# Attention with its score and weighing matmuls in blocks of eight, values stored twice, short scalings on ScalarE, memory reordered, and the third item's operands given a home of their own

## The chip, the cores and the metric

The kernel runs on one core of a Trainium2 chip. The metric is the device time of one launch in microseconds. Engines are called as in the profile: PE is TensorE, DVE is VectorE, ACT is ScalarE, POOL is GpSimd, SP is SyncE (here it only issues DMAs).

## The reference, cut to what matters

Four batch items of 512 tokens, 1024 features, all in float32. After a layer norm the result is the sum of three things: x itself, an attention with ALiBi-like bias, and a linear layer with a low-rank part chosen by a router.

```
qkv = xn @ w_qkv                       # 32 query heads, 8 key/value heads of 128
scores = einsum(q, k) * 128 ** -0.5    # 4 query heads share one key/value head
bias = -slope * sqrt(max(i - j, 0)), -inf for j > i
attn = softmax(scores + bias)
out = attn @ v, then @ w_o
ffn = xn @ W.T + b + routed low-rank part
x + out + ffn
```

## The kernel before, in words

The kernel has three stages on one core. Matrix products are done by a two-level Strassen scheme (seven products for eight), so operands are needed as sums and differences of quarters; DVE and POOL make these.

**Projection** (`project`, matmuls on line 569). It makes q, k and v for all heads and stores them in DRAM. Values of two heads are transposed and stored by `put` (lines 597 to 602), four DMAs of 32 partitions. Beside the matmuls, one call of `beside` at a time, `weights_put_by` (from line 784) loads pieces of the weights through ACT's queue, makes sums of them on DVE or POOL (line 827) and stores them through SP's queue (line 836). `pause(n)` in it lets n turns go by. The order of PE, SP, DVE and POOL is that of the program.

**Attention** (`attend`). A unit is one batch item and one key/value head: 32 units, four steps T each, 128 steps (`STEPS`). All engines and SP's queue work in program order, so the loop over T from line 1217 is the schedule. In step T:

- `scores(T)` (line 1047): four score matmuls of 128 query rows (32 positions of four heads) against 32 to 512 keys, lines 1053 on PE. Each has one of four PSUM banks. DVE adds the bias and takes the row's extreme (line 1058, frees the bank), ACT takes the exponential and its sum (line 1061).
- `scaled(T - 1)` (line 1071): the four probability rows are multiplied by the inverse of their sums, on POOL. Of the four, two are long (288 to 512) and two short (32 to 256).
- `turn(T - 2)`: DVE transposes the step's probabilities in blocks of 32 (line 1084).
- `weigh(T - 6)` (line 1113): probabilities times values, 24 rounds' matmuls of 32 rows of the array each, four at a time (line 1100). The results of a unit stand in four PSUM banks.
- every four steps `settle` (line 1120) copies them out on ACT (line 1127).
- `aside(beside, ...)` and `aside(below, ...)` take the next of the operand sums that the last stage needs: `outer_sums` on POOL, `middle_sums` on DVE where `kept` (items 1 and 2) or of `os` (5, 6, 3), on POOL for 7 and 4. They end in DMA stores to `s_d` through SP's queue (lines 1172 to 1186), for the last pair of heads partly through POOL's (line 1168). `below` advances by one or two sums a step in turn.
- `load` brings q and k of the next unit; `values` (line 1030) brings v of this unit, four DMAs of 32 partitions from the same source, since the weighing needs v on each quarter of the partitions.

In step 112 the first operands of the last stage are loaded (`front[0]`), in step 130 the second item's (`second_home`), and `begin` puts the first matmuls of the last stage between the last weighings. After the loop come the sums of the last pair.

**Last stage** (`finish`, matmuls on line 1371). 49 items (7 outer times 7 inner products); an item needs four operand quarters `sa00` to `sa11`, its weights `w` and sums of them (`tokens`, `weights`). Operands of item n + 2 are loaded while item n runs (`beside`, slots 2 to 6). Item 0 is done without the inner scheme; ACT copies its results into the tile `u` (line 1394).

Pools lie in memory as stacks. The pool `b` of the attention and the pool `c2` of the last stage start at the same place, so where a tag stands in the list of line 1215 decides which tile of the attention a tile of the last stage must wait for. Offsets in words of a partition, worked out from the sizes in the code, before: ot1 16128 to 18176, vy to 20224, pty to 24832; in `c2` t4 15872 to 17152, u 17152 to 19200.

Of the kernel before, what the change touches and what calls it, by code (L numbers as in the profile page):

```python
# [66 lines left out]
def kernel(  # L67
# [58 lines left out]
    v_d = {(i, h): scratch(f"v{i}_{h}", [2, 32, P // 32, NT, D]) for i in range(B) for h in range(0, NKV, 2)}  # L126
# [238 lines left out]
    def project(attention):  # L365
# [5 lines left out]
        with pool("a") as sb, tc.tile_pool(name="stats", bufs=2, reuse_waits="tile") as stats:  # L371
# [182 lines left out]
            def item(st, i, acc):  # L554
# [30 lines left out]
                def put(t, row, col):  # L585
                    bi = 2 * p + row
                    if kind == "q":
                        src = t.rearrange("p a b -> p (a b)").rearrange("p (j f) -> p j f", f=2 * C)
                        dst = q_d[bi, h].rearrange("p j g k -> p j (g k)")
                        nc.sync.dma_start(out=dst[:, :, ts(col, 2 * C)], in_=src)  # L590
                    elif col == 0:
                        nc.sync.dma_start(out=k_d[bi, h], in_=t)
                    else:
                        for j in range(2):
                            tr = bank("tr", f"v_{n}_{j}")
                            for c in range(NT):
                                nc.tensor.transpose(tr[:, ts(c, P)], t[:, j, ts(c, P)], ident)
                            nc.scalar.copy(t[:, j], tr)
                        dst = v_d[bi, h].rearrange("j k g c d -> g k j (c d)")
                        in_while(4, lambda: [  # L600
                            nc.sync.dma_start(out=dst[g], in_=t[ts(g, 32)]) for g in range(P // 32)
                        ])
# [181 lines left out]
            def weights_put_by(turn):  # L784
# [31 lines left out]
                for n in range(turn, len(pieces), 3):  # L816
                    key, eng = pieces[n], (GP, V)[n % 2]
                    if len(key) == 2 and key[1] in SUMMED:
                        while not put_by >= {(key[0], e, j) for e in range(2) for j in range(2)}:
                            yield  # L820
                    w = load(key)
                    yield from pause(8)
                    for k, u, v in ((0, 1, 0), (1, 3, 1), (3, 3, 0), (2, 2, 3)):
                        while busy(eng):
                            yield
                        taken[eng] = pace[2]
                        pin(sub(eng, w[:, k], w[:, u], w[:, v]))
# [143 lines left out]
    def attend(front, begin):  # L971
# [3 lines left out]
        with ExitStack() as stack:  # L975
# [177 lines left out]
            def middle_sums(p, h, which, of, t, kept):  # L1153
# [27 lines left out]
                for k in range(g):  # L1181
                    if kept:
                        nc.sync.dma_start(out=d[k][:, 1], in_=s3[:, k])
                    else:
                        queue.dma_start(out=d[k][:, :4], in_=a[:, k].rearrange("p e r k -> p (e r) k"))
                    queue.dma_start(out=d[k][:, 4:], in_=m[:, :3, k])
                yield

            beside, below = deque(), deque()
# [71 lines left out]
            p, h = last  # L1261
            cuts = [(ALL, slice(HS, S)), (ALL, slice(0, HS))]
# [157 lines left out]
    def finish(sb, homes, ops, begun):  # L1420
# [16 lines left out]
        for tags, shape, n in (  # L1437
            ("x", [NP, 2, HS], 4), ("btb", [DOUT], 1), ("um", [NP, S], 1), ("lw", [12, P], 1),
            ("r4", [2, NP, HS], 8), ("t4", [KB, P], 2), ("u", [2, NP, HS], 2),
            ("m1 m5 m6", [HS], 2), ("wz", [2 * KB, HS], 1), ("sa10z sa11z", [KB, HS], 1),  # L1440
            ("s2 s4", [KB, HS], 2), ("t3", [KB, P], 2),
# [203 lines left out]
        def beside(n, slot):  # L1645
# [57 lines left out]
    homes, begun = [], {}  # L1703
    ops = {n: None for n in range(2)}

    def lay(home, k):

        for tag, shape in (
# [3 lines left out]
            home.tile([P, *shape], F32, tag=tag, name=f"lay_{tag}_{k}")  # L1712
# [10 lines left out]
    def second_home(o):  # L1723
# [7 lines left out]
        bring(1, "w", (0, 1))  # L1731

# [59 lines left out]
```

## Time and profile before

| | us |
|---|---|
| median of 3 runs | 2530.95 (2528.68 to 2532.22) |
| the profiled execution | 2529.27 |
| its span | 2527.5 |

| engine | busy us | share of the span |
|---|---|---|
| PE | 2450.1 | 97% |
| weight loads (PEld) | 2082.3 | 82% |
| DVE | 1802.9 | 71% |
| POOL | 1929.3 | 76% |
| ACT | 516.0 | 20% |

DMA moved 681.90 MB, 270 GB/s on average. The projection takes the first 1143 us of the span, the attention lasts to some 1722, the last stage from there.

A busy share is the mean over stages with different limits, so stretches of the span are read one by one. In a line of instructions, the name behind "<-" in brackets is what ended the idle time ahead of the instruction. A matmul in float32 stands as two records (two passes). The DMA share is the mean busy share of 16 DMA engines; it is over 1 where packets overlap. The granted clock is 1.00 at full speed.

### The profile page before, as it was taken

The numbers are of one execution on the slowest core, as the hardware profiler recorded it, in microseconds if no ns is written. First come the engines' busy times: TensorE is split into PE (matmuls) and PEld (weight loads), VectorE is DVE, ScalarE is ACT, GpSimd is POOL, SyncE is SP. The second block draws the span as 40 slices with busy tenths as digits, with TensorE's granted clock in tenths as the row PEclk, the third lists the DMA queues.
The fourth block names the chain that finished last, engine by engine and source line by source line (L and its number), as shares of the span: only waits on it lengthen the run. The fifth ranks groups of instructions, "written<-read, shape, count | busy, mean of one in ns | idle before, by whom it ended". The sixth has DMA issues, their size and how long they took to land.

```text
span 2527.5 us, 44178 instructions
## 1 busy us (share of the span) xinstructions
PE 2450.1 (97%) x16096; PEld 2082.3 (82%) x16096; DVE 1802.9 (71%) x3586; ACT 516.0 (20%) x1558; POOL 1929.3 (76%) x2078
## 2 busy tenths in 40 slices
PE   7999999999999999999999999997999999999999
PEld 6878888888888888887777777775888888888887
DVE  7776677778666676757899998975765666656574
ACT  3111111110000000116666666641000000000000
POOL 4578787887688898875999999975775667747583
PEclk9999999999999999999999999998999999999999
DMA  4389998878977777746899999999887877879884
GB/s 146 109 246 318 281 323 253 271 220 245 323 226 241 217 243 223 247 136 183 248 319 326 319 331 320 321 304 356 317 317 268 327 288 289 307 267 329 312 325 149
DMA packets 513834, 681.90 MB, mean 270 GB/s; under 512 B 155817, under 2 KB 424489, under 8 KB 499410
## 3 DMA queue, kind: packets, MB, share of 16 engines
q1 hardware_dynamic: 441554, 591.64, 71.5%
q10 hardware_dynamic: 70752, 82.85, 9.9%
q0 software_dynamic: 1312, 4.59, 0.5%
q8 instruction: 128, 2.10, 0.3%
q14 instruction: 88, 0.72, 0.1%
HBM read 417.89 MB, written 261.10 MB: 269 GB/s over the span
## 4 chain that ended last, share of the span: by engine, by line
PE 67%; DMA 3%; POOL 2%; DVE 1%; SPq 1%; issue 1%; ACT 0%; ACTq 0%; DVEq 0%; POOLq 0%
PE pc L1371 16%; PE po L1100 11%; PE psc L1053 10%; PE pd L1371 8%; PE pc_q L569 7%; PE pa L1371 4%; PE pd_q L569 3%; PE pc_kv L569 3%; PE pa_q L569 2%; PE pd_kv L569 2%; DMA sa<-s 1%; PE pa_kv L569 1%; POOL t L140 1%; POOL ti_q L140 1%; PE pc L1635 1%
## 5 line engine op out<-in xcount | busy, mean ns | idle before, releaser
L1100 PE MATMUL po<-pt,v 32*128 32x256 f32 (+7 forms) x6144 | 300.1, 334 | 5.1 <-DMA v<-v 4.4
L1061 ACT ACTIVATE p<-p,low 128x512 f32<-128x512 f32 (+15 forms) x512 | 261.4, 517 | 203.7 <-DVE low L1058 195.7
L1100 PEld LDWEIGHTS po<-pt,v 32*128 32x128 f32 x6144 | 266.1, 186 | 36.3 <-issue 23.7
L1073 POOL TENSOR_SCALAR p<-p,tot 128x512 f32<-128x512 f32 (+15 forms) x512 | 264.3, 534 | 41.3 <-DVE tot L1069 40.8
L1053 PE MATMUL psc<-k,q 128*128 128x512 f32 (+15 forms) x1024 | 279.4, 417 | 3.0 <-DVE low L1058 2.5
L140 POOL TENSOR_TENSOR t<-w 128x640 f32<-128x640 f32 x95 | 187.9, 1978 | 120.9 <-DMA w<-m 54.6
L1058 DVE CUSTOM_DVE_ANT_0 p<-psc,bias 128x512 f32<-128x512 f32 (+15 forms) x512 | 205.6, 435 | 69.5 <-PE psc L1053 66.1
L1053 PEld LDWEIGHTS psc<-k,q 128*128 128x128 f32 x1024 | 171.5, 191 | 96.6 <-issue 55.8
L140 POOL TENSOR_TENSOR t<-w,t 128x640 f32<-128x640 f32 x95 | 194.8, 2051 | 33.9 <-PE pc L1371 30.2
L140 POOL TENSOR_TENSOR wr<-wr 128x256 f32<-128x256 f32 x220 | 174.6, 795 | 47.2 <-DMA wr<-in_w_o_dram 21.6
L569 PE MATMUL pc_q<-xi,ti_q 128*128 128x256 f32 x640 | 167.6, 385 | 3.0 <-DVE q L137 2.7
L1084 DVE STREAM_TRANSPOSE pt<-p 128x1088 f32<-128x1088 f32 x128 | 167.0, 1305 | 1.7 <-POOL p L1073 1.7
L140 POOL TENSOR_TENSOR ti_q<-w_q 128x256 f32<-128x256 f32 x128 | 105.3, 822 | 67.7 <-PE pc_q L569 37.4
L140 DVE TENSOR_TENSOR wr<-wr 128x256 f32<-128x256 f32 x220 | 139.5, 634 | 14.0 <-DMA wr<-in_wt_dram 9.1
L569 PEld LDWEIGHTS pc_q<-xi,ti_q 128*128 128x128 f32 x640 | 121.4, 192 | 24.3 <-issue 4.9
L569 PE MATMUL pd_q<-xi,ti_q 128*128 128x256 f32 x448 | 117.6, 386 | 14.6 <-POOL ti_q L140 14.6
L179 ACT COPY m<-pc 128x256 f32<-128x256 f32 x30 | 11.2, 372 | 564.1 <-PE pc L1371 545.1
L1371 PE MATMUL pc<-s,t 128*128 128x256 f32 x480 | 113.3, 384 | 10.5 <-DVE m L137 10.5
L140 POOL TENSOR_TENSOR ti_q<-to_q 128x256 f32<-128x256 f32 x96 | 76.8, 800 | 47.5 <-PE pc_q L569 45.0
L1371 PE MATMUL pc<-sa,w 128*128 128x256 f32 x480 | 112.1, 381 | 0.1
L1371 PEld LDWEIGHTS pc<-s,t 128*128 128x128 f32 x480 | 92.4, 193 | 23.6 <-issue 10.9
L1371 PE MATMUL pd<-s,t 128*128 128x256 f32 x480 | 111.5, 379 | 0.0
(344 smaller groups left out, 5731.1 us busy)
## 6 DMA issues: line engine op xcount, KB each, us to landing
sa<-s SPq DMA_DIRECT2D x98, 640.0 KB, 7.9
s<-ot SPq DMA_DIRECT2D x107, 384.0 KB, 6.1
m<-wr SPq DMA_DIRECT2D x70, 512.0 KB, 4.1
w<-m SPq DMA_DIRECT2D x28, 1280.0 KB, 8.1
w_q<-in_w_qkv_dram SPq DMA_DIRECT2D x16, 2048.0 KB, 11.3
q<-q SPq DMA_DIRECT2D x32, 1024.0 KB, 5.7
v<-v SPq DMA_DIRECT2D x128, 256.0 KB, 5.9
s<-os SPq DMA_DIRECT2D x45, 512.0 KB, 6.1
```

Of the source, the lines that this page charges most:

```text
L140: return eng.tensor_tensor(dst, u, v, ALU.subtract)
L179: nc.scalar.copy(dst, alike(src, dst))
L569: nc.tensor.matmul(dst, ops_w[m][:, c, :], XI[i][m][:, c, :], start=start and c == 0, stop=c == 1, skip_group_check=True,)
L1053: nc.tensor.matmul(sc[:, :n], Q[u][:, n // C - 1].rearrange("p g k -> p (g k)"), K[u][:, :n], start=True, stop=True,)
L1058: nc.vector.tensor_tensor_reduce(row, sc[:, :n], bias[p, h][:, S - n :], -SCALE, BIG, ALU.add, ALU.min, low)
L1061: nc.scalar.activation(row, row, AF.Exp, bias=low, scale=-1.0, accum_out=TOT[T][:, k : k + 1])
L1073: nc.gpsimd.tensor_scalar(row, row, TOT[T][:, k : k + 1], 1.0, ALU.mult, ALU.mult)
L1084: nc.vector.transpose(dst, PR.pop(T).rearrange("p s (t k) -> p s t k", k=C))
L1100: nc.tensor.matmul(PO[u, g][:, to : to + n * C].rearrange("p (n k) -> p n k", k=C), V[u][ts(g, C), b % G * NT + b // G], x[:, :, :C], star ...
L1371: nc.tensor.matmul(bk, w[:, k], x[:, k], start=start and k == 0, stop=stop and k == KB - 1, skip_group_check=True,)
L1635: nc.tensor.matmul(bk, low["w"][:, c, d], low["u"][:, p, ts(r, HS)], start=start, stop=False, skip_group_check=True,)
```

## The change

Eight edits, all in one step:

1. Weighing: inside the 128 steps nothing is weighed in even steps, and two steps' weighings are done in odd ones, behind that step's scores. On PE two steps' scores (eight matmuls) stand together, then two steps' weighings.
2. Values are written to DRAM twice, one copy behind the other, and `values` issues two DMAs of 64 partitions (2 KB pieces) for four of 32.
3. In `scaled` the two short rows of a step go to ACT, the long ones stay on POOL.
4. The sums of items 1 and 2 go from DVE (`beside`) to POOL (`below`), and `below` advances by two sums in each step.
5. The tags of pool `b` are reordered, and the bias of the low-rank part is 256 words longer, so that tiles of the last stage lie over other tiles: now pty 12288 to 16896, vy to 18944; t4 16128 to 17408, u 17408 to 19456.
6. The last pair's sums of (5, 6, 3) and (7, 4) go to a tile in pty's place (`spare`), and their stores to SP's queue.
7. Item 2 of the last stage gets weights and `sa10`, `sa11` in a pool of its own (`c1z`); its weights and one quarter are loaded in step 130 and no longer at the start of the last stage.
8. In `weights_put_by` two of the four turns of pause behind the sums go to the pause between load and sums (8, 4 become 10, 2).

```diff
-    v_d = {(i, h): scratch(f"v{i}_{h}", [2, 32, P // 32, NT, D]) ...}
+    v_d = {(i, h): scratch(f"v{i}_{h}", [2, 32, P // 32, 2, NT, D]) ...}
...
-                        dst = v_d[bi, h].rearrange("j k g c d -> g k j (c d)")
+                        dst = v_d[bi, h].rearrange("w k g j c d -> g k w (j c d)")
                         in_while(4, lambda: [
-                            nc.sync.dma_start(out=dst[g], in_=t[ts(g, 32)]) for g in range(P // 32)
+                            nc.sync.dma_start(
+                                out=dst[g],
+                                in_=t[ts(g, 32)].rearrange("k j n -> k (j n)").unsqueeze(1)
+                                .to_broadcast([32, 2, S * 2]),
+                            ) for g in range(P // 32)
                         ])
...
-                    yield from pause(8)
+                    yield from pause(10)
...
-                    yield from pause(4)
+                    yield from pause(2)
...
-                src = v_d[2 * p + bi, h - h % 2][h % 2].rearrange("k g c d -> k (g c) d")
-                for g in range(G):
-                    nc.sync.dma_start(out=V[u][ts(g, C)], in_=src)
+                src = v_d[2 * p + bi, h - h % 2].rearrange("w k g j c d -> j (w k) g (c d)")[h % 2]
+                for e in range(2):
+                    nc.sync.dma_start(
+                        out=V[u][ts(e, 2 * C)].rearrange("k (g c) d -> k g (c d)", g=G), in_=src
+                    )
...
-                    nc.gpsimd.tensor_scalar(
-                        row, row, TOT[T][:, k : k + 1], 1.0, ALU.mult, ALU.mult
-                    )
+                    by = TOT[T][:, k : k + 1]
+                    if k % 2:
+                        nc.scalar.activation(row, row, AF.Identity, scale=by)
+                    else:
+                        nc.gpsimd.tensor_scalar(row, row, by, 1.0, ALU.mult, ALU.mult)
...
-                m = buf(f"ot{which[0]}", f"ot_{n}").rearrange("p (s g) k -> p s g k", g=g)
+                m = spare.pop(which[0]) if (p, h) == last and which[0] in spare else buf(
+                    f"ot{which[0]}", f"ot_{n}"
+                )
+                m = m.rearrange("p (s g) k -> p s g k", g=g)
...
-                eng = nc.gpsimd if of == "o" and not kept else nc.vector
+                eng = nc.gpsimd if of == "o" else nc.vector
-                queue = nc.gpsimd if (p, h) == last and not kept else nc.sync
...
-            for tag in "o ot7 ot5 os ot1 p vx vy ptx pty".split():
+            for tag in "o os pty vy ot7 ot5 ot1 p vx ptx".split():
...
-                        beside.append(middle_sums(p, h, (1, 2), "o", O[u], True))
+                        below.append(middle_sums(p, h, (1, 2), "o", O[u], True))
...
-                weigh(T - 6)
+                for k in range(T - 7, T - 5) if T % 2 and T < STEPS else [T - 6] if T >= STEPS else []:
+                    weigh(k)
                 aside(beside, 1 if T < STEPS else 4)
-                aside(below, 1 + T % 2 if T < STEPS else 4)
+                aside(below, 2 if T < STEPS else 4)
...
+            rest = sb.tile([P, 15, HS], F32, tag="pty", name="spare")
+            spare.update({5: rest[:, :9], 7: rest[:, 9:]})
...
-            self.home, self.third = homes[n % 2], homes[n % 3]
+            self.home, self.third = homes[n % 2], thirds[n % 3]
...
-            ("x", [NP, 2, HS], 4), ("btb", [DOUT], 1), ...
+            ("x", [NP, 2, HS], 4), ("btb", [DOUT + HS], 1), ...
...
-            ("m1 m5 m6", [HS], 2), ("wz", [2 * KB, HS], 1), ("sa10z sa11z", [KB, HS], 1),
-            ("s2 s4", [KB, HS], 2), ("t3", [KB, P], 2),
+            ("m1 m5 m6", [HS], 2), ("s2 s4", [KB, HS], 2), ("t3", [KB, P], 2),
...
-                {2: lambda: o.load(1, 0), 3: lambda: (o.load(1, 1), o.load_weights()),
+                {2: lambda: n and o.load(1, 0), 3: lambda: (o.load(1, 1), n and o.load_weights()),
...
         bring(1, "w", (0, 1))
+        lay(ctx.enter_context(pool("c1z", side="right")), "z")
+        bring(2, "w", (1, 0))
```

More of the change, by code (lines that the diff above doesn't have):

```diff
@@ L125 @@
     k_d = {(i, h): scratch(f"k{i}_{h}", [P, 2, S]) for i in range(B) for h in range(0, NKV, 2)}
-    v_d = {(i, h): scratch(f"v{i}_{h}", [2, 32, P // 32, NT, D]) for i in range(B) for h in range(0, NKV, 2)}
+    v_d = {(i, h): scratch(f"v{i}_{h}", [2, 32, P // 32, 2, NT, D]) for i in range(B) for h in range(0, NKV, 2)}
     s_d = {i: scratch(f"s{i}", [P, 7, NP, 2, KB, HS]) for i in OUTER}
@@ L1184, in middle_sums @@
                     else:
-                        queue.dma_start(out=d[k][:, :4], in_=a[:, k].rearrange("p e r k -> p (e r) k"))
-                    queue.dma_start(out=d[k][:, 4:], in_=m[:, :3, k])
+                        nc.sync.dma_start(out=d[k][:, :4], in_=a[:, k].rearrange("p e r k -> p (e r) k"))
+                    nc.sync.dma_start(out=d[k][:, 4:], in_=m[:, :3, k])
                 yield
-            beside, below = deque(), deque()
+            beside, below, spare = deque(), deque(), {}
             def aside(steps, times):
@@ L1437, in finish @@
         for tags, shape, n in (
-            ("x", [NP, 2, HS], 4), ("btb", [DOUT], 1), ("um", [NP, S], 1), ("lw", [12, P], 1),
+            ("x", [NP, 2, HS], 4), ("btb", [DOUT + HS], 1), ("um", [NP, S], 1), ("lw", [12, P], 1),
             ("r4", [2, NP, HS], 8), ("t4", [KB, P], 2), ("u", [2, NP, HS], 2),
-            ("m1 m5 m6", [HS], 2), ("wz", [2 * KB, HS], 1), ("sa10z sa11z", [KB, HS], 1),
-            ("s2 s4", [KB, HS], 2), ("t3", [KB, P], 2),
+            ("m1 m5 m6", [HS], 2), ("s2 s4", [KB, HS], 2), ("t3", [KB, P], 2),
         ):
@@ L1702 @@
     psum = ctx.enter_context(pool("psum", space=bass.MemoryType.PSUM))
-    homes, begun = [], {}
-    ops = {n: None for n in range(2)}
+    homes, thirds, begun = [], [], {}
+    ops = {n: None for n in range(3)}
     def lay(home, k):
+        thirds.append(home)
         for tag, shape in (
@@ L1711, in lay @@
         ):
-            home.tile([P, *shape], F32, tag=tag, name=f"lay_{tag}_{k}")
+            if k != "z" or tag[-1] == k:
+                home.tile([P, *shape], F32, tag=tag, name=f"lay_{tag}_{k}")
     def bring(n, *parts):
```

## The prediction

> **What bounds the kernel now.** I read the busy time by stretches first. Its columns are the stretch, its length, the busy time of PE, of the weight loads, of DVE, ACT and POOL, then granted clock, DMA share and GB/s.
>
> ```profile
> core 0: us, PE busy (x) PEld busy (x) DVE busy (x) ACT busy (x) POOL busy (x), PEclk, DMA share, GB/s
> 1160.00:1234.70 74.70, 74.70 (x980) 58.69 (x976) 59.64 (x189) 47.36 (x162) 52.20 (x85) 1.00 0.63 185
> 1234.70:1581.40 346.70, 346.70 (x4475) 270.18 (x4471) 314.37 (x881) 214.36 (x729) 344.87 (x439) 1.00 1.03 323
> 1634.84:1662.93 28.09, 23.56 (x228) 17.77 (x224) 15.82 (x45) 11.32 (x37) 17.39 (x24) 0.82 1.05 362
> 1697.00:1765.41 68.41, 50.37 (x456) 41.92 (x449) 36.96 (x39) 6.36 (x20) 37.89 (x35) 0.88 1.01 343
> 1765.41:2527.00 761.59, 755.77 (x3556) 664.64 (x3556) 483.56 (x501) 23.56 (x62) 493.98 (x233) 1.00 0.80 292
> ```
>
> In the attention (second and third line) three things are full at once: PE, POOL (344.87 of 346.7) and the DMA engines (share 1.03). The last stage (bottom line) is PE alone. Two short stretches between lose time and clock. The chain of what ended last says which of the three sets the pace; these eight pieces are one unit (one batch item and head pair, four steps):
>
> ```profile
> 1302.97 2.09 PE po L1100 x48
> 1305.06 2.25 PE psc L1053 x8
> 1307.31 2.12 PE po L1100 x48
> 1309.43 2.09 PE psc L1053 x8
> 1311.52 2.33 PE po L1100 x48
> 1313.86 2.03 PE psc L1053 x8
> 1315.89 2.39 PE po L1100 x47
> 1318.28 2.03 PE psc L1053 x8
> ```
>
> Scores and weighings alternate without a gap: 17.34 us a unit. Before 1234.7, with POOL 70% busy and DMA at 0.63, a unit takes the same 17.34, so PE sets it. Next the PE timeline, where the stalls stand in brackets with what ended them:
>
> ```profile
> 1650.18 6.91 PE L1100 MATMUL po<-pt,v 32*128 32x256 f32 x48 [4.44 <-DMA v<-v]
> ...
> 1745.78 4.20 PE L1371 MATMUL pc<-s,t 128*128 128x256 f32 x10 [10.51 <-DVE m L137]
> ...
> 1760.67 4.63 PE L1371 MATMUL pc<-sa10y,t 128*128 128x256 f32 x10 [6.38 <-DVE m L137]
> ```
>
> The last view is DMA: 3.5 us in which value loads ran (1309 to 1312.5), 5 us of stores (1317 to 1322), and ten pairs of units (1234.7 to 1581.4):
>
> ```profile
> DMA packets 156, 0.77 MB, mean 221 GB/s; under 512 B 45, under 2 KB 63, under 8 KB 64
> ...
> DMA packets 1874, 1.88 MB, mean 377 GB/s; under 512 B 64, under 2 KB 1871, under 8 KB 1871
> ...
> DMA packets 74930, 111.87 MB, mean 323 GB/s; under 512 B 4792, under 2 KB 67193, under 8 KB 69753
> ```
>
> **PE: two scores, then two weighings.** From the starts of the records: inside a run a pass of N columns starts its successor N/1.2 ns later (512: 428). A unit streams 8 x 1.813 = 14.50 us; 2.84 is something else. At a change from scores to weighing the last pass takes 96 to 152 ns too long and the first round 107; at a change back 110 to 140 (335 behind a 32-column round) and 107. Per unit: 8 x 107 + 442 + 696 = 1.99 us. After the change half of the changes remain: 428 + 194 + 250 = 0.87. The new neighbours cost what like neighbours cost inside runs today (a long pass behind a 64-column one 0.12, behind a 32-column one 0.17, the two others 0.01 together): 0.30. So 1.99 - 1.17 = **0.82 us a unit**, 16.52 us. Weighings 0 to 121 are paired, 30.5 units: 25.0 us if PE stays the bound.
>
> The odd step's scores now wait directly for DVE's reductions of the even step to free four banks. DVE empties a bank in 0.18 to 0.68 us behind each score, about as fast as PE fills them; behind the wait stand both weighings, which have four steps of margin. I take 0 (upper bound 0.1 a unit).
>
> **POOL.** Per pair of units (34.68 us now) it loses 16 short scalings (rows 290 to 470 ns, 3.06 a unit, 6.1) and gains 4 sums of 128x512. Rows: long scalings 4.77 a unit, a sum 1.27 (o<-o,o, 1269 ns). After: 2 x 4.77 + 16 x 1.27 = 29.8, less 32 overlapping starts of 25 ns, 29.0. The same count today gives 29.8 against 34.5 busy: the 4.7 more are pushes by DVE's eight sums (6.2 us by themselves). Four of those stay (3.6): 29.0 + 2.7 = 31.7, or 32.6 if they push by all they take. That fits under PE's 33.04, with little room.
>
> The Trainium skill (SBUF — State Buffer, Two separate sides) says that a DVE operation with two SBUF inputs and a GpSimd operation take turns as whole instructions. Its figure would make the push the full 3.6, so the sum would be 32.6 and not 31.7.
>
> **ACT** gets 8 short scalings a unit. Nearest row, its own exponentials of those lengths: 3.25 us on top of 10.7, 14.0 of 16.5: hidden. They queue behind the step's exponentials; DVE's transpose of that tile comes a step later. **DVE** loses 4.1 us a pair (27.4 left): free.
>
> **DMA decides how much of this is kept.** A pair moves 11.19 MB. Its 2.10 MB of values at 221 GB/s take 9.5 us, the other 9.09 MB at the stores' 377 take 24.1: 33.6 us, 16.8 a unit, above PE's 16.52. Bounds: 33.0 (PE binds) to 34.3 (what is busy today but for the few gaps). Does the value load get faster? It goes from four loads of 32 partitions to two of 64, same bytes, 2 KB pieces in place of 8 KB. No load of 64 partitions stands in the trace; from below, v's own rate, 221; from above, the packets of q over 128 partitions (8 KB in 311 ns by 16 engines, 421 GB/s), which would bring v to 5.0 and the pair to 29.1. I take v's own row, the nearest: still half the partitions at a time.
>
> The Trainium skill (SBUF — State Buffer, Door 1: The DMA port swizzle) speaks against this edit: partitions 0 to 63 reach the same 8 of 16 ports as 0 to 31. By it v keeps its rate and the pair its 33.6; by the row of q it would be 29.1. No run here shows it yet.
>
> So: the first 4 units (DMA share 0.63) win 0.82 each, 3.3; the other 26.5 win 17.34 - 16.8 = 0.54, 14.3. The stall at 1645: that unit took 28.09, 10.75 too long, of which 28.09 x (1 - 0.82) = 5.1 is lost clock. The operand loads of 3.2 MB behind it stay a debt of the DMA engines, but the values are due one score later and SP issues 2 for 4 (2.87 us there), so the wait comes in pieces: only the clock, 5.1. **Attention: 22.7 us.**
>
> **The turn to the last stage.** The 10.51 us: ACT's first copy into u waited 22.25 us for stores s<-ot, because u (word 17152 of its pool) lay in ot1 (16128 to 18176). Now u is at 17408, in vy (16896 to 18944), free with the last weighing. The 6.38: t4 lay in os, whose last stores went through POOL's queue (issued 1744 to 1755, landing 1753 to 1770); now it lies in pty and vy. The last pair's ot5 and ot7 go to pty's place, so the 7.4 and 6.1 us waits of DVE for s<-ot go. PE could start item 2 at 1730.8 + 7 x 2.16 = 1745.9, not 1765.4. What is late next is DMA: 22.46 MB went in 1700 to 1765.4 at 343 GB/s. Item 2 still needs all but the third operand quarter (0.65) and item 3's share (some 3.9): 17.9 MB, 52.1 us, **13.3 us less**. Bounds: 19.5 (PE) and 8 (SP's ten further stores, 0.4 to 1.3 us each, stand ahead of the last quarter; POOL is rid of them, 0.74 to 0.83 us each). Item 2's weights and quarter move ahead of the last sums' stores on SP; these have 20 us.
>
> **Projection.** Values are stored twice: 64 stores grow from 128 to 256 KB, at a DMA share of 0.75 to 0.85 and off the chain; 0, at most 3 lost. Weight sums start two turns later behind their load and are stored with two turns less: at 691 us PE stood 7.7 us behind POOL's 12.5 us wait for such a load. I take 1 us won (bounds 3 lost, 3 won).
>
> **Sum.** 22.7 + 13.3 + 1 = 37. The profiled execution took 2529.27 (span 2527.5), 1.7 below the median of the runs, 2530.95. Forecast 2529.3 - 37 = **2492 us**.
>
> **Rivals.** (a) v comes faster: PE binds, 25.0 + 10.75, 16 at the turn, 1: 53, **2477**. For it: slow packets only where v runs. (b) POOL binds: a sum at the mean of its rows today (233.1/153 = 1.52): 16 x 1.52 + 9.5 - 0.8 = 33.1 plus part of the push, 34.1 a pair, 17.05 a unit: 3.3 + 7.7 + 5.1 + 13.3 + 1 = 30, **2499**. (c) The turn stays bound by DMA and SP: 8, with DMA's upper bound in the attention 3.3 + 5.0 + 5.1: 21, **2508**. (d) Slower: POOL's moved sums take turns with DVE so badly that each costs 1.79 (row os<-o,os): 28.6 + 9.5 - 0.8 = 37.3 a pair, +1.3 a unit x 26.5 = +35, against 3.3 + 13.3 + 1: **2546**; it decides from a unit of 18.0, 1.71 us a sum. Against it: half of DVE's sums are gone. (e) The changes of mode come back as waits and the turn moves no less: within 0.2%.
>
> **Chances.** Forecast 0.50, (a) 0.22, (b) 0.11, (c) 0.08, (d) 0.06, (e) 0.03. A measurement of this kernel tells 0.2% (5 us) from no change. Forecast with its bounds: 2477 (PE binds, 19.5 at the turn) to 2511; with (a) 2474 to 2511 leaves out (d), (e) and a tail of (a). Faster 0.91, same 0.03, slower 0.06.
>
> **What would show it.** Score runs of 16 and weighing runs of 96 matmuls; a unit between 16.5 and 17.1 us; PE gaps before psc or po ended by q or v, not by POOL; DMA share still about 1 and values at some 221 GB/s (near 400 would be (a)); no half clock at 1650; item 2 about 13 us sooner behind the last weighing. Wrong: a unit over 17.2, sums on POOL over 1.71 us, or new PE waits at the turn.

## The result, and the profile after

The changed kernel takes 2594.28 us (median of four runs, 2590.05 to 2597.33) against 2530.56: a ratio of 1.0251, 95% interval 1.0233 to 1.0269. Forecast were 2492 us and a range to 2511. It is slower by 64 us where 37 less were forecast.

The profiled execution (2597.33, span 2595.6) is 68.1 longer than the one before. By the first score matmul and the last weighing, which part the stages: the projection takes **46.9** us more (first score at 1187.7, before 1140.8), the attention **15.2** more (595.9 for 580.7), the rest **5.9** more (811.9 for 806.0). No stage is shorter. The stretches of after, first (projection; ten pairs of units; last weighing to the third item's first matmul; the rest); the columns are those of the first view in the prediction (length, busy time of the five engines, granted clock, DMA share, GB/s):

```profile
core 0: us, PE busy (x) PEld busy (x) DVE busy (x) ACT busy (x) POOL busy (x), PEclk, DMA share, GB/s
20.00:1187.70 1167.70, 1098.59 (x5184) 953.30 (x5185) 773.44 (x1629) 134.51 (x300) 869.52 (x1083) 0.97 0.76 234
1299.40:1659.00 359.60, 338.80 (x4481) 266.72 (x4481) 280.74 (x840) 262.51 (x890) 316.86 (x320) 0.98 1.02 312
1783.70:1831.79 48.09, 25.33 (x100) 20.32 (x100) 16.58 (x20) 2.32 (x8) 14.71 (x10) 0.81 1.01 337
1831.80:2595.00 763.20, 758.17 (x3556) 665.62 (x3556) 479.14 (x503) 23.58 (x62) 487.35 (x230) 0.99 0.79 291
```

The same stretches of before, where the prediction had not shown them (projection; last weighing to the third item's first matmul):

```profile
20.00:1140.80 1120.80, 1086.21 (x5184) 943.98 (x5185) 784.02 (x1629) 134.28 (x300) 872.78 (x1083) 0.99 0.76 236
1721.50:1765.41 43.91, 26.36 (x100) 21.43 (x101) 21.68 (x24) 2.25 (x8) 18.42 (x18) 0.82 1.00 354
```

In the projection PE is idle 69 us where it was idle 35, and the granted clock is lower (0.97 for 0.99). Ten pairs of units (second line of after) now take 359.6 us, before 346.7; PE is idle 20.8 of them, POOL 42.7. So neither is the bound there, and the DMA engines move 312 GB/s where they moved 323. The turn has grown from 43.9 to 48.1.

What PE waits for in the attention stands in the chain of waits (start, length, what):

```profile
1296.17 3.22 issue
1299.39 7.13 PE psc L1059 x16
1306.53 4.28 PE po L1108 x96
...
1317.26 1.27 SPq L1195
1318.57 1.57 SPq L1196
1320.18 2.86 SPq L1195
1323.09 1.49 SPq L1196
1324.68 0.86 SPq L1009
1325.58 10.45 DMA q<-q
1336.16 4.24 PE psc L1059 x16
1340.40 4.24 PE po L1108 x96
```

The first lines: PE stood for 3.22 us, and the 16 score matmuls behind that took 7.13 us where the later ones take 4.24: the granted clock was 0.50 in the first 2.6 us of them and 0.64 in the 4.5 behind. (x16 and x96 show that the blocks of eight are there.) The others: SP issues stores of sums (L1195 and L1196, in `middle_sums`) one behind the other for 7 us, then k (L1009) and q, and q takes 10.45 us to land. SP's own waits say what held the stores; the columns are the total in us over these ten pairs, how many and the longest:

```profile
SPq L1195 <- POOL o L140: 79.6, 10, 8.6
SPq L1193 <- POOL ot L140: 28.3, 10, 5.5
```

SP issues in order. Before, it stood 51.1 and 32.5 us, for DVE's sums. At the turn two PE stalls are left, of 13.08 us behind DVE and of 8.30 us behind a load; the second view is DVE's:

```profile
1811.92 4.61 PE L1384 MATMUL pc<-s,t 128*128 128x256 f32 x10 [13.08 <-DVE m L137]
1831.79 3.78 PE L1384 MATMUL pc<-sa,w 128*128 128x256 f32 x8 [8.30 <-DMA sa<-s]
```
```profile
1809.94 1.49 DVE L140 TENSOR_TENSOR s<-s,sa 128x1280 f32<-128x1280 f32 x1 [14.98 <-DMA s<-ot]
```

The old wait of 22.25 us for u is gone as forecast, but a sum of the second item now waits 15 us for the stores of the tile that it lies over.

### The profile page after: what moved, and what is told of

The parts are those of the page before. It is cut to its first block, busy times and chain, and to the rows that moved or that the text cites. A ratio compares the mean times of both kernels' runs of the same rounds, so it can differ in the third digit from the quotient of the medians.

```text
span 2595.6 us, 44213 instructions
## 1 busy us (share of the span) xinstructions
PE 2446.9 (94%) x16096; PEld 2083.1 (80%) x16096; DVE 1731.7 (67%) x3522; ACT 592.0 (23%) x1814; POOL 1876.0 (72%) x1876
## 4 chain that ended last, share of the span: by engine, by line
PE 56%; DMA 7%; SPq 4%; POOL 2%; ACT 2%; issue 2%; DVE 2%; ACTq 0%; DVEq 0%; POOLq 0%
PE pc L1384 15%; PE pd L1384 8%; PE pc_q L569 6%; PE psc L1059 6%; PE po L1108 5%; PE pa L1384 4%; DMA q<-q 4%; PE pc_kv L569 3%; PE pd_q L569 3%; PE pd_kv L569 2%; SPq L1196 2%; PE pa_q L569 2%; SPq L1195 1%; ACT p L1067 1%; PE pa_kv L569 1%
## 5 line engine op out<-in xcount | busy, mean ns | idle before, releaser
L140 POOL TENSOR_TENSOR t<-w 128x640 f32<-128x640 f32 x95 | 182.4, 1920 | 154.0 <-DMA w<-m 87.3
L1108 PE MATMUL po<-pt,v 32*128 32x256 f32 (+7 forms) x6144 | 278.5, 331 | 4.7 <-DMA v<-v 4.3
L1108 PEld LDWEIGHTS po<-pt,v 32*128 32x128 f32 x6144 | 254.6, 186 | 27.2 <-ACT p L1067 9.6
L1083 POOL TENSOR_SCALAR p<-p,tot 128x512 f32<-128x512 f32 (+7 forms) x256 | 150.7, 602 | 91.8 <-DVE tot L1075 90.2
L179 ACT COPY m<-pc 128x256 f32<-128x256 f32 x30 | 11.2, 372 | 609.1 <-PE pc L1384 592.6
L1384 PE MATMUL pc<-s,t 128*128 128x256 f32 x480 | 113.7, 385 | 13.1 <-DVE m L137 13.1
L569 PEld LDWEIGHTS pd_q<-xi,ti_q 128*128 128x128 f32 x448 | 86.0, 195 | 49.2 <-POOL ti_q L140 37.7
L140 DVE TENSOR_TENSOR s<-s,sa 128x1280 f32<-128x1280 f32 x48 | 89.7, 1869 | 37.1 <-DMA sa<-s 21.8
```

Source lines behind the costliest of these rows:

```text
L140: return eng.tensor_tensor(dst, u, v, ALU.subtract)
L179: nc.scalar.copy(dst, alike(src, dst))
L569: nc.tensor.matmul(dst, ops_w[m][:, c, :], XI[i][m][:, c, :], start=start and c == 0, stop=c == 1, skip_group_check=True,)
L1083: nc.gpsimd.tensor_scalar(row, row, by, 1.0, ALU.mult, ALU.mult)
L1108: nc.tensor.matmul(PO[u, g][:, to : to + n * C].rearrange("p (n k) -> p n k", k=C), V[u][ts(g, C), b % G * NT + b // G], x[:, :, :C], star ...
L1384: nc.tensor.matmul(bk, w[:, k], x[:, k], start=start and k == 0, stop=stop and k == KB - 1, skip_group_check=True,)
```

## The experiments

Two theories of the projection: **A**, the doubled value stores cost it; **B**, the changed pauses do. In a later run A is parted into **O**, the doubled stores changed the order of ScalarE's instructions, and the transfers themselves (called B again there). Two of the attention: **S**, SP comes late to the query loads because stores ahead of them wait for sums; **D**, the DMA engines bind, as forecast, only dearer since each stall costs clock. Of the turn: **Q**, SP's queue; **R**, the transfers. Totals are medians; in brackets is the ratio to the kernel before in the same job with its interval.

### Which edit took the projection's time

"Values once" undoes edit 2 (`v_d`, `put` and `values` as before), "old pauses" edit 8:

```diff
-                    yield from pause(10)
+                    yield from pause(8)
...
-                    yield from pause(2)
+                    yield from pause(4)
```

**After, values once.** 

> The kernel after, with the values stored once and loaded by four loads of 32 partitions, as before. Theory A (the doubled value stores and the 2 KB pieces cost the time): the stalls that come every 142 us of the projection go, the first score stands at 1143 to 1150 us as before and not at 1190, a pair of units in the attention takes 0.8 us less than the 35.9 of after (values 8.8 us of DMA time for 9.6), total 2535 to 2550 us. Theory B (the changed pauses of the weight sums cost it: SP reaches their stores before POOL has the sums, and everything on SP's queue stands): the first score stays at about 1190 us, total 2580 to 2594.

2547.36 us (1.0056, 1.0038 to 1.0074); first score at 1134.7; attention 599.5. Theory A holds for the projection. The pair of units got no shorter, against the 0.8 us of that theory.

**After, old pauses.** 

> The kernel after, with the pauses of the weight sums put back to 8 turns behind the load and 4 ahead of the store; values still in two copies. Theory A (value stores): nothing comes back, first score at 1185 to 1190 us, total 2588 to 2597. Theory B (pauses): first score at 1143 to 1150 us, total 2545 to 2555.

2596.63 us (1.0251, 1.0233 to 1.0269), first score at 1182.7, 5 us ahead of after's 1187.7, where B had some 40. Theory B falls.

**Before, with values twice alone.** 

> The kernel before, with the values stored twice and loaded by two loads of 64 partitions, nothing else. Theory A: first score at about 1185 to 1190 us in place of 1142.7, total 2570 to 2585. Theory B: first score at 1143 to 1146 us, total 2530 to 2541 (at most the 0.8 us a pair that the values take longer comes on top).

2572.92 us (1.0165, 1.0150 to 1.0180); first score at 1184.2, 43.4 later. The edit costs this by itself. Its attention is 583.3, 2.6 more, so the new loads cost little and win nothing.

**After, values once and old pauses.** 

> The kernel after with both undone: values once, pauses 8 and 4. Both theories: first score at 1143 us. What is left against before is then the attention and the turn: a pair of units at 35.1 us (after less 0.8), so about +5 to +8 us there, and +3 at the turn: total 2535 to 2545 us. If the DMA engines do not bound the attention but SP's stores that wait for POOL's moved sums do, a pair stays at 35.9 and the total is 2548 or more.

2550.08 us (1.0074, 1.0059 to 1.0089), first score at 1140.7. Between these two runs with values once the new pauses are worth 6 us in the projection; between the two with the values twice they cost 5 (1182.7 to 1187.7). What is left against before lies in the attention (592.8), and the total is over 2548, which the expectation gave to SP's stores.

**How it costs that.** ScalarE's queue, before, around 550 us: it copies out of PSUM and issues loads of weight pieces (wr):

```profile
548.81 0.58 ACT L362 COPY umT<-ptr_u 64x512 f32<-64x512 f32 x1 [15.15 <-PE ptr_u L359]
548.95 0.90 ACTq L794 DMA_DIRECT2D wr<-in_w_o_dram  x2
549.97 0.96 ACTq L801 DMA_DIRECT2D wr<-t  x2
557.49 0.37 ACT L179 COPY q<-pc_q 128x256 f32<-128x256 f32 x1 [8.10 <-PE pc_q L569]
```

The same place in the run with the values twice, and there POOL and PE:

```profile
568.97 0.58 ACT L362 COPY umT<-ptr_u 64x512 f32<-64x512 f32 x1 [15.14 <-PE ptr_u L359]
577.64 0.37 ACT L179 COPY q<-pc_q 128x256 f32<-128x256 f32 x1 [8.10 <-PE pc_q L569]
577.75 0.90 ACTq L798 DMA_DIRECT2D wr<-in_w_o_dram  x2
```
```profile
581.89 2.33 POOL L140 TENSOR_TENSOR wr<-wr 128x256 f32<-128x256 f32 x3 [11.56 <-DMA wr<-in_w_o_dram]
```
```profile
584.96 2.08 PE L569 MATMUL pd_q<-xi,ti_q 128*128 128x256 f32 x4 [7.39 <-POOL ti_q L140]
```

The copy that waits 8.1 us for PE now stands ahead of the loads. They are issued 8.8 us behind umT and not 0.1, POOL's weight sum waits 11.56 us for one, POOL is in order, and PE stands 7.39 us for POOL's operand sums. (The clock granted in the projection is 0.97 in the row of after, 0.99 before.) Nobody edited ScalarE's order. It is not written out by hand in this stage (those of PE, SP, DVE and POOL are): a planner puts it together from its own estimate of when things are ready. That it takes the wr buffer, whose store stands behind the larger ones on SP, to come free later is argued; that the order is another is read from the two traces. Copies moved ahead of loads at four places (131, 276, 428 and 577 us), and behind each stands a stall of 6.2 to 10.5 us. The large stall of before, 7.67 us at 691, is of the same kind: there the copy stood ahead already. Two more stalls with the values twice, 10.25 us at 720 and 4.84 at 858 (before, the 7.67 and none), stand where ScalarE's order is that of before.

That the places agree is no proof, as bytes and order changed together. So the order was fixed and the bytes were changed alone:

```diff
+    def hold(ins):
+        if loaded[0] is not None:
+            tc.add_manual_dep(ins.ins, loaded[0], NO_SYNC, reason="behind the last load")
+        return ins
...
+                def held(ins):
+                    pin(ins)
+                    loaded[0] = ins.ins.name
+                    return ins
...
-                nc.scalar.copy(dst, alike(src, dst))
+                hold(nc.scalar.copy(dst, alike(src, dst)))
```

Each wr load goes through `held`, and the copies of lines 179 and 302 through `hold`: an order within ScalarE, no wait.

**Before, copies held behind the loads.** 

> The kernel before, values once, with one addition: in the projection each copy of ScalarE out of PSUM is bound behind the last load of the weight sums that was traced before it, so that ScalarE's order can't change with the size of the stores. It is the base for the run with the values twice; PE's, DVE's, POOL's and SP's orders are those of before. Both theories: first score at 1136 to 1146 us, total 2523 to 2536.

2519.72 us (0.9955, 0.9940 to 0.9971), first score at 1130.5: 10 us less in the projection from the order alone; the stall of before at 691 us is 3.29 here.

**The same with values twice.** 

> The same with the values stored twice (and loaded by two loads of 64 partitions): the orders of all five engines are those of its base, only the stores and loads of the values differ. Theory O (the doubled stores cost the projection its 41 to 47 us through the order: with them the planned order has copies of ScalarE, which wait 8 to 23 us for PE, ahead of weight loads at four places, and four of the new stalls stand at these places): first score within 8 us of the base, total at most 10 above it. Theory B (the 8.4 MB more and the slow stores themselves delay loads and sums): first score 30 to 45 us above the base, total 30 to 50 above it.

2537.95 us (1.0030, 1.0015 to 1.0045), first score at 1147.3. Neither theory alone: at one and the same order the doubled stores cost 16.8 us of projection (18.2 of the total); with the planner's order they had cost 43.4. So the transfers make 17 of 43 and the order some 27 (a difference of two differences, if the transfers cost the same under both orders). What makes the 17, the bytes or that each store leaves 32 partitions, was not parted.

### What the attention lost

**After, values once, by one load over 128 partitions.**

```diff
-                for g in range(G):
-                    nc.sync.dma_start(out=V[u][ts(g, C)], in_=src)
+                nc.sync.dma_start(
+                    out=V[u].rearrange("k n d -> k (n d)"),
+                    in_=src.rearrange("k n d -> k (n d)").unsqueeze(0).to_broadcast([G, C, NT * G * D]),
+                )
```

> The kernel after with the values stored once, and each unit's values loaded by one DMA over all 128 partitions that reads the stored copy four times, in place of four loads of 32. Theory D (the DMA engines bound the attention; values are slow because a load touches a quarter or half of the partitions): values go at the rate of q's packets (8 KB in 0.31 to 0.37 us, not 0.61), a pair's DMA work falls from about 34.3 to 30 us, below PE's 33.0; pairs of units at 33.0 throughout, the attention 595 to about 560 us, total about 2505 to 2520 us. Theory S (SP, which issues in order, comes to the query loads late, because the stores ahead of them wait for POOL's moved sums): pairs stay at about 36 with stalls that q ends, total 2540 to 2550. If it is not the partitions that make values slow, packets stay at 0.6 us and the time at 2545.

2724.67 us (1.0782, 1.0754 to 1.0810); pairs of 36 to 48 us. A miss, and no test of either theory: the packets are fast (309 ns), but only four go at a time. Its DMA view in 4 us in which one load ran:

```profile
DMA  3033033033033015015013113113103303303303
DMA packets 52, 0.43 MB, mean 106 GB/s; under 512 B 0, under 2 KB 0, under 8 KB 0
```

8 KB in 309 ns by four engines is 106 GB/s. The source's outermost dimension has four entries (the copy read four times). The Trainium skill (DMA: Bandwidth & Descriptors, Why a DMA increments its semaphore by 16 and not by 1) says that a DMA runs on the largest number of engines up to 16 that divides the slowest dimension of both sides; four agrees.

**After, values once, each step weighed by itself.** The loop of edit 1 is `weigh(T - 6)` again.

> The kernel after with the values as before (stored once, four loads) and each step weighed by itself again, in place of two scores and then two weighings; all else as after. Theory D: PE is slower than the DMA engines again (a pair 34.7 against 34.3), so it never runs into a stall over 3 us and keeps its full clock: pairs at 34.7, attention 579 to 584 us in place of 599, total 2530 to 2536 us: the faster PE order made the attention slower. Theory S: the stores still wait for POOL, q is still issued 10 us ahead, stalls stay: attention 590 or more, total 2540 or more.

2552.53 us (1.0090, 1.0071 to 1.0110); pairs of 35 to 42, attention 606.8. D falls: a PE no faster than before stalls as much.

**After, values once, stores a turn later.**

```diff
+                def put():
+                    for k in range(g):
...
+                late.append(put) if turns[0] < STEPS else put()
...
+                while late:
+                    late.popleft()()
```

`put` holds the stores that stood behind the last sum; `late` is emptied in the loop over T, behind `load` and `values`.

> The kernel after with the values as before (once, four loads), and the stores of POOL's and DVE's sums issued one step later, behind that step's loads, so that SP no longer stands before a sum that is not done. Theory S: q is issued 15 to 20 us ahead, the stalls go, pairs at 33.0 to 34.3, attention 560 to 575 us, total 2515 to 2530. Theory D: SP is free, but the transfers take as long: pairs still 35.5 to 36 on average, total 2540 to 2550.

2529.92 us (1.0002, 0.9983 to 1.0021); attention 578.7. Pairs run at 33.0 to 37.3. The query loads of the first unit of each pair are now issued some 21 us ahead (before that 10 to 17), those of the second still 9 to 12: eight stores stand ahead of them. The result lies between the two theories.

**The same, stores held to the next even step, and the turn's loads split.**

```diff
-                while late:
+                while late and (T % 2 == 0 or T >= STEPS):
...
+                if T == STEPS + 2:
+                    aside(beside, 99)
+                    front[4]()
```

`front[4]` has the second half of `second_home`: the second item's weights and (0, 1), and the third item's loads.

> The kernel after with values once, the sums' stores held back to the next even step, so that every unit's query load stands ahead of them on SP (in the run before, the odd units' still stood behind eight), and at the turn the stores of the pair before the last ahead of the second item's weights, its quarter (0,1) and the third item's loads. Theory S (SP's order is what keeps the attention from PE's pace): both units of a pair get q 17 us or more ahead, pairs at 33.0 to 33.5 throughout, attention 558 to 568 us in place of 578.7. Theory D (under that the DMA engines bind, as forecast at 33.6 to 34.3 a pair): q is issued early but lands late, stalls in lumps remain, attention 572 to 580. The turn: the 12.3 us stall falls to about 5 if the stores' place on SP made it; it stays if the transfers did. Totals: 2495 to 2510 with S and the turn, 2510 to 2520 with D and the turn, 2525 with neither.

2509.35 us (0.9927, 0.9914 to 0.9939). Each of the ten pairs takes 33.0 us; attention 557.7. S holds, and D's bound of 33.6 us was too high, as the same bytes go in 33.03:

```profile
1234.00:1564.30 330.30, 330.30 (x4481) 263.01 (x4481) 283.86 (x841) 261.90 (x891) 318.61 (x321) 1.00 1.05 339
```

At the turn the stores' place won nothing: the 12.3 us stall went, but PE now stands 9.71, 4.87, 2.37 and 3.68 us, mostly for weights and a quarter, 20.6 us in all, and from the last weighing to the end it is 813.1 us for 813.7.

**Before, with pairs of steps and the short chunks on ScalarE alone** (edits 1 and 3).

> The kernel before with two parts alone: two scores and then two weighings, and the short chunks scaled on ScalarE. The sums stay on VectorE, the values in one copy, the turn as it was. Theory S with the moved sums as its cause: SP's order stays that of before, q is issued 11 to 14 us ahead, PE runs at 33.0 a pair until the transfers hold it: pairs at 33.0 to 34.3, attention 565 to 575 us in place of 580.7, total 2515 to 2526. If the order of eight blocks by itself brings q late (the lead falls to about 10 and stalls of 3 us appear), pairs at 35.5 or more, attention 590, total 2535 or more.

2505.49 us (0.9905, 0.9890 to 0.9920); pairs 33.0, attention 557.1.

**The same with the moved sums** (edit 4).

```diff
-                eng = nc.gpsimd if of == "o" and not kept else nc.vector
+                eng = nc.gpsimd if of == "o" else nc.vector
-                        beside.append(middle_sums(p, h, (1, 2), "o", O[u], True))
+                        below.append(middle_sums(p, h, (1, 2), "o", O[u], True))
-                aside(below, 1 + T % 2 if T < STEPS else 4)
+                aside(below, 2 if T < STEPS else 4)
```

> The run before with pairs and ScalarE (2505 us), and on top of it alone the moved sums: items 1 and 2's middle sums on POOL behind the pair's others, two steps of the sums a turn. Theory S, moved sums as the cause: SP stands before POOL's sums again, stalls ended by q come back every second pair, pairs 35.5 to 36 on average, attention 590 to 600 us in place of 557, total 2538 to 2550. If the moved sums are harmless and one of the other edits of after (layout, pauses) spoiled the attention: pairs stay at 33.0, total 2503 to 2510.

2549.12 us (1.0084, 1.0067 to 1.0102); attention 592.0: the moved sums alone cost 35 us of attention. Ten pairs, in 360 us for 330:

```profile
1234.00:1594.00 360.00, 340.25 (x4504) 267.66 (x4496) 280.10 (x841) 262.81 (x893) 316.00 (x322) 0.97 1.01 313
```

SP's queue in the run without them, around the query of a pair's second unit (issue, the time that it held SP, what):

```profile
1402.81 0.37 SPq L1005 DMA_DIRECT2D k<-k  x1
1403.22 0.43 SPq L1006 DMA_DIRECT2D q<-q  x1
1407.35 0.37 SPq L1187 DMA_DIRECT2D s<-os  x1
1407.77 0.51 SPq L1188 DMA_DIRECT2D s<-ot  x1
1408.32 1.30 SPq L1187 DMA_DIRECT2D s<-os  x1
```

and in the run with them, with the stall of 3.78 us that q ended:

```profile
1380.21 0.38 SPq L1187 DMA_DIRECT2D s<-os  x1
1380.63 1.47 SPq L1188 DMA_DIRECT2D s<-ot  x1
1382.15 0.69 SPq L1187 DMA_DIRECT2D s<-os  x1
1382.88 0.70 SPq L1188 DMA_DIRECT2D s<-ot  x1
1384.01 0.99 SPq L1187 DMA_DIRECT2D s<-os  x1
1385.06 2.43 SPq L1188 DMA_DIRECT2D s<-ot  x1
1387.59 1.25 SPq L1005 DMA_DIRECT2D k<-k  x1
1388.88 0.54 SPq L1006 DMA_DIRECT2D q<-q  x1
1389.52 3.10 SPq L1035 DMA_DIRECT2D v<-v  x4
1397.78 0.38 SPq L1187 DMA_DIRECT2D s<-o  x1
```
```profile
1399.67 2.78 PE L1053 MATMUL psc<-k,q 128*128 128x512 f32 x5 [3.78 <-DMA q<-q]
```

Six stores (three of 512 and three of 384 KB, 2.75 MB, 8 us at 336 GB/s) have come from behind the query to ahead of it, since two sums a step, with `beside` rid of items 1 and 2, bring these sums to their end earlier in the program. And behind the loads SP stands 5 us before a sum of POOL, in which nothing is issued. Over ten pairs the unused share of the DMA engines adds up to 11.8 us there, and to 2.7 without the moved sums (from the packets in steps of 0.25 us). That SP's order is the cause is shown by the run with the stores held to the next even step, where the sums are moved too and every pair is back at 33.0; how much each of the two costs, the stores ahead of q and the wait behind it, was not parted. How early q is issued says little by itself: without the moved sums it is 8 to 12 us from the ninth unit on, and PE never waits for q, as less stands ahead of it.

### The turn

**After, values once, third item's loads late.** `second_home` ends without `bring(2, ...)`, and slots 2 and 3 of `beside` load them for n = 0 again.

> The kernel after with the values as before, and the third item's first loads (its weights and one operand quarter) issued in the first item, as before, and not ahead of the last stores; their place stays. Theory Q (SP's queue makes the turn: these loads keep SP from 1736 to 1742.5 us, and DVE's sum for the second item waits 16 us for the stores behind them): the PE stall of 14.2 us falls to about 8, total 2540 to 2543 us. Theory R (the transfers themselves bound the turn): the same bytes come a little later, the second stall grows by what the first gives, total 2546 to 2549.

2543.03 us (1.0055, 1.0037 to 1.0072): the first stall falls from 14.19 us to 6.60 as Q has it, the second grows to 16.82 from 8.31. Nothing is won in sum: the run with values once stood at 1.0056.

**Before with the parts that had done no harm** (edits 1, 3 and 8).

> The run before with pairs and ScalarE, with the changed pauses of the weight sums (10 behind the load, 2 ahead of the store) added; values once, sums and turn as before. Two runs that differ in the pauses alone had the first score at 1134.7 and 1140.7 us, so theory: 4 to 6 us less than 2505.5, total 2499 to 2503. Rival: that difference came from elsewhere, total 2504 to 2508.

2498.33 us (0.9885, 0.9871 to 0.9898), first score at 1135.5.

**The same with the new homes** (edit 5, `spare`, `c1z`; loads and queues as before).

> The same with the new homes at the turn added (pool reordered, u and t4 over other buffers, the last pair's sums over pty, the third item's operands in a home of their own), but with the third item's loads at their old time and the last stores on POOL's queue. Theory as forecast (the old stalls of 10.6 and 5.9 us at the turn are waits for buffers, the transfers allow 13 us less): the turn 8 to 13 us shorter, total 2488 to 2493. Rival (the transfers or SP's queue bound the turn anyway): new stalls of the same sum, total 2499 to 2506.

2506.10 us (0.9911, 0.9898 to 0.9925). The new places cost 7.8 us by themselves. Where PE and DVE stand there:

```profile
1711.45 4.04 PE L1379 MATMUL pc<-s,t 128*128 128x256 f32 x10 [5.22 <-DVE m L137]
1730.89 4.57 PE L1379 MATMUL pd<-s,w 128*128 128x256 f32 x10 [15.40 <-DVE s L140]
```
```profile
1729.35 1.49 DVE L140 TENSOR_TENSOR s<-sa,s 128x1280 f32<-128x1280 f32 x1 [17.71 <-DMA s<-ot]
```

**The same with the last stores on SP** (edit 6's other half).

> The same with the last pair's ten stores on SP's queue too. Theory Q (SP's queue is the turn's limit: it took 12 us to issue these ten in an earlier run, and the second item's quarter stood behind them): 6 to 12 us more than the run with the stores on POOL's queue. Rival (the transfers bound it): within 3 us of it.

2506.70 us (0.9915, 0.9902 to 0.9929): the same. Q falls here. DVE's wait of 17.71 us is 4.82 here, and PE stands 15.44 us behind a load of the third item instead: the wait moved and the sum stayed.

The stalls of over 1 us at the turn, up to the third item's first matmul, add up to 16.5 to 18.2 us in each kernel with the old homes and to 20.6 to 24.0 in each with the new ones, whatever is loaded first. From the last weighing to that matmul it is 44.23 us without the new homes and 49.66 with them, both at a full DMA share:

```profile
1690.70:1734.93 44.23, 26.69 (x102) 21.84 (x101) 19.63 (x23) 2.29 (x8) 17.93 (x17) 0.77 1.01 355
```
```profile
1692.50:1742.16 49.66, 26.15 (x101) 21.45 (x101) 23.85 (x23) 2.31 (x8) 20.17 (x17) 0.79 1.00 334
```

### The best version

**Edits 1, 3 and 8, and the copies held behind the loads.**

> The fastest kernel so far (before with pairs, short chunks on ScalarE and the changed pauses, 2498 us) with the copies of ScalarE bound behind the weight loads. The binding alone took 9.6 us off the kernel before; if that adds to the rest, 2486 to 2491 us; if the changed pauses had already taken the same stalls, 2494 to 2500.

2486.56 us (0.9825, 0.9811 to 0.9838): 43.8 below the kernel before. First score at 1123.8, pairs 33.0, the turn 46.1 us (43.9 in before).

## Why the prediction was wrong, step by step

**"Values are stored twice: ... off the chain; 0, at most 3 lost" failed worst.** Measured: 43.4 us by itself, 47 in the sum. The prediction asked whether there is room for the bytes (a share of 0.75 to 0.85) and not who waits for what stands behind these stores on SP. It never asked about ScalarE's order in the projection, which no line of the diff touches. Of the 43, the order made some 27 and the transfers 17. **The pauses** were costed at 1 us won; without the doubled stores they won 6 to 7 (1140.7 to 1134.7, and 2505.5 to 2498.3), and with them they cost 5; that the win comes from a load with longer to land is argued.

**"PE: ... 0.82 us a unit" was right.** A unit takes 16.515 us where 16.52 was worked out (33.03 a pair, in the runs without SP's stalls). **POOL** was right: 31.7 us a pair forecast, 31.7 measured in after (316.86 in ten), so the rivals (b) and (d) fall. The 32.6 that came out of the Trainium skill's rule of turns (SBUF — State Buffer, Two separate sides) is further off. ACT took 13.1 a unit (14.0 forecast).

**"DMA: 33.6 us a pair" was 2% too high, and not the bound.** The 11.1 to 11.2 MB of a pair went in 33.03 us at 336 to 339 GB/s in three kernels, as rival (a) had it (PE binds), but not because values came faster. The sum took two rates, each from a stretch of few microseconds, one after the other; that loads and stores overlap is the likely error, and not shown. Nor does the DMA share tell the bound: it is 1.02 in after and 1.04 to 1.05 in these three, where ten pairs are 8% shorter. The attention of the run with edits 1 and 3 won 23.6 us, close to the 22.7, but by another sum: 25 from PE, while the stall behind the values (5.7 us at 1625, before 4.4) was not gone as forecast; that run keeps the four loads.

**What was left out in the attention is the price of the moved sums: 35 us.** They were costed as busy time of POOL and DVE only. The diff moves stores with them, and the prediction did not follow SP's order past the query load. Its own list of proofs had a place for that ("PE gaps before psc or po ended by q or v"); it took such gaps for the sign of a full DMA engine, where the run with the stores put back showed a queue in the wrong order.

**Does the value load get faster? No, as forecast.** In 3.5 us of after with hardly anything but values:

```profile
DMA packets 373, 0.73 MB, mean 209 GB/s; under 512 B 16, under 2 KB 16, under 8 KB 373
```

64 partitions at a time gave 209 GB/s, 32 gave 221. The rule of the Trainium skill (SBUF — State Buffer, Door 1: The DMA port swizzle) agrees with that, and it speaks against edit 2 as a whole.

**The turn: "13.3 us less" failed, it grew by 4** (43.9 to 48.1 us). The old waits for u and t4 went, but sums of the second item now lie over ot5 and ot1 (by the sizes in the code), and one waits 15 us in after, and 18 with the new homes alone, for stores s<-ot. "What is late next is DMA" was right; that only 17.9 MB would still have to go was not: in the stretch that begins some 21 us ahead of the last weighing's end and reaches to the third item's first matmul, after moved 22.4 MB, before 22.5. Whether the tile that is waited for or the order of the bytes sets the new sum was not parted: from the last weighing on, transfers go at some 330 to 340 GB/s with the new homes and at 350 to 360 with the old, and why is open.

**The sum.** -1, -22.7 and -13.3 were forecast; +46.9, +15.2 and +5.9 came. Rival (d) had the sign, but not the cause. Of the attention's +15.2, edits 1, 3 and 4 together make 11.3 (592.0 in the run with them alone); the other 4 lie within the spread of after and its variants with values once, old pauses, both, or the third item late (592.8 to 603.0).

## What to carry to other kernels

Work that moves to another engine takes its stores along: write out the in-order queue that issues them, before and after, and count the bytes that come ahead of the next load that someone waits for. Where a planner orders an engine, compare the planned orders of both versions, also on engines that the diff does not touch; a larger transfer is enough to change them, and it can cost more than the bytes. And try the parts of a change alone: three of the eight edits held the gain, and the one that looked free cost most.

## What the runs showed of the hardware beyond what was expected

- One load over 128 partitions whose source has an outermost dimension of four entries ran on four DMA engines: 106 GB/s, packets of 8 KB at 309 ns.
- The DMA engines kept 339 GB/s over 330 us with loads and stores mixed, although values alone go at 209 to 221.
- A PE stall of 3.22 us was enough for slow matmuls behind it: 16 scores in 7.13 us for 4.24, at a granted clock of 0.50 in the first 2.6 us. In the run with the moved sums alone a stall of 2.56 us (at 1471) was enough: 0.56 in the 3.8 us behind it.
